# Where u times D joins the state sums of a selective scan: diagonal blocks on TensorE, or a VectorE step

## The chip, the cores and the metric

The kernel runs on one core of a Trainium2 chip. Times are device microseconds (us) of that core. The engines are TensorE (PE, with its weight loads shown as PEld), VectorE (DVE), ScalarE (ACT), GpSimd (POOL) and SyncE (SP), which issues the DMAs. SBUF is the memory on the chip, PSUM the banks into which TensorE writes its products.

## The reference

A decoder layer on x of 16 batches x 256 positions x 512 features, in three stages, each followed by a residual add and a layer norm: a selective scan, a cross-attention of 16 heads, and a gated feed-forward network (FFN) with ternary weights. What the change touches is the end of the scan stage. For each batch, with 1024 channels d, 16 states n and 256 positions l:

```
hs   = silu(conv(x W_in_states))              # (d, l), called u in the kernel
dA   = exp(A[d,n] * dt[d,l])
s    = dA * s + dt * B[n,l] * hs              # scan over l, for every d and n
y    = sum over n of s[d,n,l] * C[n,l]
y    = y + hs * D[d]
y    = y * silu(gate)
out  = y W_out
```

The line `y + hs * D` is the one whose place moves.

## The kernel before

**Tiling.** Batches go one after the other in the code (`prep`, `scan`, `attn`, `ffn` for each b), but the instructions of several batches lie beside each other: a planner orders them. The 1024 channels are eight tiles of 128 (d = 0 to 7). In the scan a tile is split into four groups g of 32 channels; a group spreads its 32 channels times 4 state rows over 128 partitions, and 4 state columns times 256 positions over the free dimension, so that one buffer h of 128x1024 holds all 16 states of 32 channels.

**One group of the scan** (the loop over g in `scan`): a DMA fetches dt and dt*u into a buffer `dtr` (L654); GpSimd multiplies B into it (`first`, through the helper `product`, L233; some of batch 0's on VectorE, L661); ScalarE makes the decays into a PSUM buffer `dA` (L668, twice two of them); VectorE runs the recurrence (L672, two scans of 128x512); GpSimd multiplies by C (`weigh`, L233 again). So a tile takes eight GpSimd products and eight VectorE scans.

**The end of a tile.** Task `sums` on TensorE takes a PSUM bank `pb` and adds up: first four blocks of 32x32, one for each group, whose diagonal holds D (`diag`, L694), times u; then 16 products with the selector `sel`, which add the state rows and columns of the four h buffers (L697). It frees the four h buffers. The first sums wait for the last `weigh`. Task `gate` on VectorE multiplies the bank by the gate z into u (L705) and frees the bank. After four tiles the output projection reads u (L736). `diag` is made once, in the setup (L326).

A float32 product appears in the trace as two records, so a tile has 8 records of L694 and 32 of L697.

**Order.** Every step is a task with an engine, a due time and an estimated duration: `task(t, engine, us, fn, after, take, free)`. The function `run` simulates the five queues (PE, DVE, ACT, POOL, SP) in these planner units and issues, for an idle engine, the ready task with the earliest due time whose buffers are free, as long as that due time is within AHEAD of the earliest task not begun. The chip then executes each engine's queue strictly in the order so written. The due times are sums of constants at the head of the file (SCAN, WEIGHP, SUMP and GATE for the scan; PREP, PSTEP, SOFT and SSTEP for the stage before; OUT0, ATT, SLAG, NORM and LNF for the attention; FFN and FDN for the FFN; WQ0 and WQ for the start and step of the 24 weight-quantising tasks, L439 and L441). Batches are due 32 units (NSL) apart. Buffers come from rings of fixed size (h has 7, dtr 4, dA 2, five general PSUM banks).

Other lines that are named later: L517 is the convolution's step on VectorE, L520 its end; L845 the row maxima of the attention; L889 its exponentials on ScalarE; L896 its weighted values; L830 its scores; L491 and L544 projections; L763 and L766 the attention's projections and their bias; L1013, L1023 and L1025 the FFN's upper half, L1086 and L1089 its lower; L458 and L459 the layer norm's statistics.

Of the kernel before, what the change touches and what calls it, by code (L numbers as in the profile page):

```python
# [10 lines left out]
F32 = mybir.dt.float32  # L11
# [4 lines left out]
ALU = mybir.AluOpType  # L16
# [4 lines left out]
P = 128  # L21
L = 256
H = 512
DI = 1024
NS = 16
NDT = DI // P
# [13 lines left out]
NB4 = 4  # L40
DB = P // NB4
# [1 line left out]

PREP = -24.16
SOFT = -7.09
SSTEP = 9.0
VUNITS = 24
GATE = -0.34
OUT0 = 25.01
OUT1 = 34.11  # L50
PSTEP = 2.02
TSP = 15.44
BCP = 9.29
KP = 34.45
QP = 37.76
VP = -3.68
SUMP = 0.16
WEIGHP = 1.88
FSTEP = 0.74
FUP = -0.18  # L60
BACK = 0.59

SHIFT = [(0, 0, 0, 0, 0, 0)] * 16
FDN = 14.54
LNF = 7.28
ATT = 39.73
SLAG = 7.79
GSTEP = 3.93
SCAN = -0.29
NORM = 81.05  # L70
FFN = 98.49
WQ = 3.57
WQ0 = 21.99
WS = 0.66
WS0 = 14.23
AHEAD = 12.29
HOP = 0.2
RINGS = {
    "xT": 2, "win": 2, "wr": 1, "wout": 1, "u": 4, "tmp": 2, "z": 2, "s": 3, "ts": 1, "bc": 1, "bcr": 3, "dtr": 4, "h": 7,
# [7 lines left out]
def decoder_kernel(ctx, tc, x, xT, ctx_in, mask, winT, wdtT, wbcT, wdpT, woutT, dvec, wqkvT, bqk, bv, wguT, wdnT, out):  # L87
    nc = tc.nc
# [16 lines left out]
    def const(shape, dt, s):  # L105
        return cp.tile(shape, dt, tag=s, name=s)
# [37 lines left out]
    def task(t, eng, us, fn, after=(), take=(), free=(), kb=0):  # L144
        if any(h.tag == "ps" for h in free) and eng in ("DVE", "ACT"):
            t -= BACK
        k = Task()
        k.t, k.i, k.eng, k.us, k.fn, k.take, k.free, k.kb = t, len(tasks), eng, us, fn, take, free, kb
        k.then, k.begun = [], False
        k.left = len(after)  # L150
        for p in after:
            p.then.append(k)
        for h in take:
            h.first = k
        for h in free:
            h.users += 1
        tasks.append(k)
        return k
# [104 lines left out]
    def cut(t, a, b):  # L263
        return t.rearrange("p (a b) -> p a b", a=a, b=b)
# [4 lines left out]
    dv = cut(free["pT"][0][:, : NDT * 23], NDT, 23)  # L269
# [14 lines left out]
    sel = const([P, DB], F32, "sel")  # L284
# [36 lines left out]

    sel4 = const([P, 2 * NS], F32, "sel4")
    nc.vector.tensor_reduce(sel4, ident.rearrange("p (g m) -> p m g", m=2 * NS), AX.X, ALU.add)
    diag = const([P, NDT, 2 * NS], F32, "diag")
    for d in range(NDT):
        nc.vector.tensor_scalar(diag[:, d, :], sel4, dv[:, d, 5:6], None, ALU.mult)  # L326
    wbc_t = const([P, NDT, 2 * NS], F32, "wbc")
    wqkv_t = const([P, 2, 768], F32, "wqkv")

# [70 lines left out]
    def setup_w():  # L400
# [33 lines left out]
        for j in range(24):  # L434
            t = WQ0 + WQ * j
            h, q = Hold("hq"), Hold("fw")
# [57 lines left out]
    def prep(b):  # L494
# [9 lines left out]
        for d0 in range(0, NDT, 2):  # L504
            t = T + PREP + PSTEP * d0
            hw, t_w = load_win(t - 5, d0 * P) if b else load_win(T + PREP - 3 + 0.1 * d0, d0 * P, "h")
# [72 lines left out]
        for hf in range(2):  # L579
            t = T + SOFT + SSTEP * hf  # L580
            ds = (4 * hf, 4 * hf + 2)
# [32 lines left out]
    def scan(b):  # L614
        st = S[b]
        T = b * NSL + SHIFT[b][1]
        st["t_y"] = []
        J = NS // NB4
        if b == 0 and VUNITS:

            hb = Hold("ps", 2)

            def spread():
                for i in range(2):
                    nc.scalar.copy(hb.t[i], st["B"].t[:, i * H : (i + 1) * H])

            t_hb = task(T - 2, "ACT", 1.1, spread, (st["t_B"],), (hb,), (st["B"],))


        hx, t_x = st["xT"]  # L630
        st["z"], st["t_z"] = [], []
        for i in range(4):
            d0, t = 2 * i, T + 8 * i + GATE
            hw, t_w = load_win(t - 5, DI + d0 * P)
            pb, z = Hold("ps"), Hold("z")

            def silu(pb=pb, z=z):
                nc.vector.scalar_tensor_tensor(z.t, z.t, 1.0, pb.t, ALU.add, ALU.mult)

            m = task(t, "PE", 3.45, lambda pb=pb, hw=hw: project(pb.t, hx, hw), (t_x, t_w), (pb, z), (hx, hw))  # L640
            m = task(t, "ACT", 0.53, lambda pb=pb, z=z: nc.scalar.activation(z.t, pb.t, AF.Tanh, scale=0.5), (m,))
            st["z"].append(z)
            st["t_z"].append(task(t, "DVE", 0.61, silu, (m,), (), (pb,)))
        for d in range(NDT):
            hs, ws = [], []
            for g in range(NB4):
                k = NB4 * d + g
                t = T + k - SCAN
                hd, hh = Hold("dtr"), Hold("h")
                hs.append(hh)  # L650

                def fetch(d=d, g=g, hd=hd):
                    src = st["dtd"][d, DB * g : DB * g + DB].rearrange("c k l -> c (k l)")
                    nc.sync.dma_start(out=hd.t, in_=src.unsqueeze(1).broadcast_to([DB, NB4, 2 * L]))  # L654

                def first(hd=hd, hh=hh):
                    product(cut(hh.t, J, L), cut(st["B"].t, J, L), hd.t[:, None, L : 2 * L].broadcast_to([P, J, L]))

                def first_v(hd=hd, hh=hh):
                    for i in range(2):  # L660
                        nc.vector.tensor_tensor(  # L661
                            cut(hh.t, J, L)[:, 2 * i : 2 * i + 2, :], cut(hb.t[i], 2, L), hd.t[:, None, L : 2 * L].broadcast_to([P, 2, L]), ALU.mult
                        )

                def decay(h2, ha, hd=hd, d=d, g=g):
                    for i in range(2):
                        j = 2 * h2 + i
                        nc.scalar.activation(ha.t[:, i, 1:], hd.t[:, 1:L], AF.Exp, scale=A[:, d, g, j : j + 1])  # L668

                def run_(h2, ha, hh=hh):  # L670
                    seg = hh.t[:, 2 * h2 * L : 2 * (h2 + 1) * L]
                    nc.vector.tensor_tensor_scan(seg, ha.t.rearrange("p n l -> p (n l)"), seg, 0.0, ALU.mult, ALU.add)  # L672

                def weigh(hh=hh):
                    st["hC"] = product(hh.t, hh.t, st["C"].t)

                f = dma(t - 4, fetch, (st["t_dt"][d // 2],), (hd,), (), 256)
                if b == 0 and k % 2 and k < VUNITS:
                    p1 = task(t - 0.75, "DVE", 1.2, first_v, (f, t_hb), (hh,), (hd, hb))
                else:  # L680
                    p1 = task(t - 0.75, "POOL", 2.34, first, (f, st["t_B"]), (hh,), (hd, st["B"]))
                rs = []
                for h2 in range(2):
                    ha = Hold("dA")
                    a = task(t - 0.6 + 0.5 * h2, "ACT", 0.92, lambda h2=h2, ha=ha, f=decay: f(h2, ha), (f,), (ha,), (hd,))
                    rs.append(task(t + 0.5 * h2, "DVE", 1.14, lambda h2=h2, ha=ha, f=run_: f(h2, ha), (a, p1), (), (ha,)))
                ws.append(task(t + WEIGHP, "POOL", 2.34, weigh, tuple(rs) + (st["t_C"],), (), (st["C"],)))
            pb = Hold("ps")

            def sums(hs=hs, pb=pb, d=d):  # L690

                for g in range(NB4):
                    r = slice(DB * g, DB * g + DB)
                    nc.tensor.matmul(pb.t[r, :L], diag[r, d, :], st["u_of"](d)[r, :], start=True, stop=False, tile_position=(DB * g, DB * g))  # L694
                for j in range(J):
                    for g in range(NB4):
                        m = nc.tensor.matmul(  # L697
                            pb.t[DB * g : DB * g + DB, :L], sel, cut(hs[g].t, J, L)[:, j, :], start=False, stop=j == J - 1, tile_position=(0, DB * g)
                        )
                        if j == 0 and g < NB4 - 1:  # L700
                            after(m, st["hC"])

            def gate(pb=pb, d=d):
                u = st["u_of"](d)
                nc.vector.tensor_tensor(u, pb.t[:, :L], st["z"][d // 2].t[:, d % 2 * L : (d % 2 + 1) * L], ALU.mult)  # L705

            m = task(T + 4 * d + 4 + SUMP, "PE", 2.45, sums, tuple(ws), (pb,), tuple(hs))
            st["t_y"].append(task(T + 4 * d + 4.25 + SUMP, "DVE", 0.42, gate, (m, st["t_z"][d // 2]), (), (pb, st["z"][d // 2])))


    def attn(b):
# [81 lines left out]
        for s in range(4):  # L793
            t = T + att + SLAG + VP + 0.7 * s
            pb = Hold("ps")
# [18 lines left out]
        def heads(g):  # L814
# [69 lines left out]
            for c in range(4):  # L884
                t = T0 + c * gstep / 4 + SLAG
                hp = Hold("pT")
# [40 lines left out]
        no = (n0, n1)  # L927
        t = T + NORM + SHIFT[b][4]
        SO = tuple(t_so)
# [29 lines left out]
    def ffn(b):  # L959
# [74 lines left out]
        for t in range(2):  # L1034
# [60 lines left out]
            t_d.append([task(Et + 1, "DVE", 0.74, add, (m,), (), (pb, ho))])  # L1095
        t_e = layernorm(E + LNF, hr, t_d)
        dma(E + LNF + 0.5, lambda: nc.sync.dma_start(out=out[b].rearrange("(k p) h -> p k h", p=P), in_=x2()), tuple(t_e), (), (hr,), 512)

# [78 lines left out]
```

## Time and profile before

| | |
|---|---|
| median of 3 runs | 3010.79 us (3008.86 to 3011.28) |
| the profiled execution | 3007.98 us, of which the span of instructions is 3005.8 us |
| granted TensorE clock, mean | 0.965 |
| VectorE scans, L672 | 1024 of 1208 ns, 1223.3 us |
| GpSimd products of the scan, L233 | 1012 of 2363 ns, 2385.6 us |
| diagonal blocks, L694 | 1024 records, 84.9 us |
| sums, L697 | 4096 records, 262.0 us |
| gate, L705 | 128 of 413 ns, 52.8 us |

How to read a profile's rows: a group is "line engine operation out<-in shapes xcount | busy us, mean ns of one | idle time of the engine before them <- who ended it". Records of an engine can overlap, so busy times of groups can add up to more than an engine's busy time. A wait is written "who <- for whom: us in total, times, longest us". A row of a timeline is "start, duration, engine, line, operation, x how many in a row"; a bracket gives the idle time before it. The chain is followed back from the last instruction: at each step to what released it, or to the instruction before it on the same engine.

### The profile page before, as it was taken

To read this page: it belongs to the slowest core of one execution; us is meant where nothing else is said; L and a number is where in the kernel's file an instruction comes from. 1 tells how busy PE (TensorE), PEld (TensorE's weight loads), DVE (VectorE), ACT (ScalarE), POOL (GpSimd) and SP (SyncE) were. 2 spreads that over 40 slices of the span, in tenths; PEclk is the share of its full clock that TensorE was granted. 3 is DMA by queue.
4 is the path that set the end of the run, shared out by engine and by line. 5 is a ranking of instruction groups with operands and counts; after the bars stand their busy time and mean duration, and the time that the engine had idled before them with its cause. 6 is when DMAs were issued, how large, how long until landed. Compare 5 with 4: busy or idle time off the path is not lost.

```text
span 3005.8 us, 51881 instructions
## 1 busy us (share of the span) xinstructions
PE 2650.5 (88%) x17514; PEld 1319.4 (44%) x17514; DVE 2674.1 (89%) x4043; ACT 2334.0 (78%) x4731; POOL 2596.5 (86%) x1435
## 2 busy tenths in 40 slices
PE   6567888999989999898999989899998999999995
PEld 4333443454545445444444544444353544434333
DVE  6969888999989999898999989899999989999873
ACT  4787978787787878778787877878788787888674
POOL 3899999999898999989899998989989899999311
PEclk9787999999999999999999999999999999999998
DMA  6695776566465665746665574656646566564432
GB/s 215 222 305 182 233 224 205 188 199 206 143 218 182 204 195 171 224 138 214 193 200 186 168 224 150 216 189 196 189 157 226 165 203 193 187 203 147 125 98 71
DMA packets 363250, 567.46 MB, mean 189 GB/s; under 512 B 47316, under 2 KB 200024, under 8 KB 358888
## 3 DMA queue, kind: packets, MB, share of 16 engines
q1 hardware_dynamic: 362984, 564.16, 58.2%
q8 instruction: 137, 2.24, 0.3%
q14 instruction: 129, 1.06, 0.1%
HBM read 449.61 MB, written 114.43 MB: 188 GB/s over the span
## 4 chain that ended last, share of the span: by engine, by line
POOL 28%; PE 27%; DVE 16%; ACT 13%; issue 10%; DMA 5%; SPq 1%; POOLq 0%; ACTq 0%; DVEq 0%
POOL h L233 23%; DVE h L672 7%; PE bank L491 6%; ACT pT L889 4%; PE bank L697 4%; DVE mx L845 4%; PE av L896 3%; PE bank L830 3%; ACT dA L668 3%; PE bank L1013 3%; PE bank L763 2%; PE bank L799 2%; DMA dtr<-dtd 2%; ACT xres L469 1%; POOL s L233 1%
## 5 line engine op out<-in xcount | busy, mean ns | idle before, releaser
L672 DVE TENSOR_TENSOR_SCAN h<-dA,h 128x512 f32<-128x512 f32 x1024 | 1223.3, 1208 | 83.0 <-POOL h L233 41.2
L233 POOL TENSOR_TENSOR h<-h,bcr 128x1024 f32<-128x1024 f32 x512 | 1207.9, 2363 | 95.7 <-DVE h L672 92.9
L233 POOL TENSOR_TENSOR h<-bcr,dtr 128x1024 f32<-128x1024 f32 x500 | 1177.7, 2363 | 69.9 <-PE bank L697 63.4
L668 ACT ACTIVATE dA<-dtr,A 128x255 f32<-128x255 f32 x2048 | 963.9, 475 | 297.1 <-DVE h L672 255.6
L830 PE MATMUL bank<-qk 108*128 108x512 bf16 x2003 | 616.3, 385 | 78.9 <-DVE mx L845 44.7
L845 DVE TENSOR_REDUCE mx<-bank 128x1 f32<-128x512 f32 x1004 | 655.1, 675 | 25.8 <-PE bank L830 25.6
L889 ACT ACTIVATE pT<-bank 128x512 f32<-128x512 f32 x999 | 566.6, 590 | 119.1 <-PE bank L830 113.9
L491 PE MATMUL bank<-xT,win 128*128 128x256 f32 x1984 | 454.5, 382 | 20.4 <-DVE u L520 7.8
L896 PE MATMUL av<-pT,vaug 128*32 128x256 f32 x4096 | 336.2, 397 | 106.6 <-ACT pT L889 104.5
L491 PEld LDWEIGHTS bank<-xT,win 128*128 128x128 f32 x1984 | 377.2, 192 | 83.8 <-DVE u L520 9.5
L830 PEld LDWEIGHTS <-qk 108*128 108x128 bf16 x2048 | 179.7, 98 | 392.2 <-issue 264.2
L697 PE MATMUL bank<-h,sel 128*32 128x256 f32 x4096 | 262.0, 399 | 49.0 <-POOL h L233 48.9
L1013 PE MATMUL bank<-fw,xqT 128*128 128x512 fp8e4 x976 | 248.5, 381 | 12.5 <-DVE hq L1023 4.0
L896 PEld LDWEIGHTS av<-pT,vaug 128*32 128x32 f32 x4096 | 88.8, 109 | 356.8 <-ACT pT L889 277.9
L736 PE MATMUL bank<-wout,u 128*128 128x512 f32 x512 | 231.0, 595 | 4.9 <-DVE u L705 4.4
L697 PEld LDWEIGHTS bank<-h,sel 128*32 128x32 f32 x4096 | 124.1, 114 | 180.9 <-POOL h L233 72.2
L517 DVE SCALAR_TENSOR_TENSOR tmp<-bank,cw,tmp 128x254 f32<-128x254 f32 (+2 forms) x384 | 165.1, 468 | 7.8 <-ACT tmp L510 7.7
L1013 PEld LDWEIGHTS <-xqT 128*128 128x128 bf16 x1024 | 96.3, 98 | 151.4 <-issue 57.6
L736 PEld LDWEIGHTS bank<-wout,u 128*128 128x128 f32 x512 | 96.0, 190 | 108.5 <-issue 94.4
L1086 PE MATMUL bank<-fw,s 128*128 128x512 fp8e4 x496 | 127.0, 380 | 1.8 <-ACT s L1077 1.1
L233 POOL TENSOR_TENSOR s<-s,u 128x512 f32<-128x512 f32 x64 | 80.7, 1272 | 39.9 <-ACT s L595 39.9
L705 DVE TENSOR_TENSOR u<-bank,z 128x256 f32<-128x256 f32 x128 | 52.8, 413 | 60.9 <-PE bank L697 60.8
(157 smaller groups left out, 2961.7 us busy)
## 6 DMA issues: line engine op xcount, KB each, us to landing
dtr<-dtd SPq DMA_DIRECT2D x512, 256.0 KB
win<-in_winT SPq DMA_DIRECT2D x124, 512.0 KB
qk<-sqk SPq DMA_DIRECT2D x128, 384.0 KB
dtd<-s SPq DMA_DIRECT2D x64, 512.0 KB
wout<-in_woutT SPq DMA_DIRECT2D x32, 1024.0 KB
fw<-gu_q SPq DMA_DIRECT2D x64, 512.0 KB
sqk<-qf SPq DMA_DIRECT2D x64, 384.0 KB
bcr<-bcd SPq DMA_DIRECT2D x32, 512.0 KB
```

What stands on the lines that cost most here:

```text
L233: return nc.gpsimd.tensor_tensor(out, a, b, ALU.mult)
L491: nc.tensor.matmul(ps_t[:, i * L : (i + 1) * L], ws[:, k, i * P : (i + 1) * P], xt[:, k, :], start=k == 0, stop=k == 3)
L517: nc.vector.scalar_tensor_tensor(zi, pb.t[:, i * L : (i + 1) * L - s], cw[:, d0 + i, j : j + 1], zi, ALU.mult, ALU.add)
L668: nc.scalar.activation(ha.t[:, i, 1:], hd.t[:, 1:L], AF.Exp, scale=A[:, d, g, j : j + 1])
L672: nc.vector.tensor_tensor_scan(seg, ha.t.rearrange("p n l -> p (n l)"), seg, 0.0, ALU.mult, ALU.add)
L697: m = nc.tensor.matmul(pb.t[DB * g : DB * g + DB, :L], sel, cut(hs[g].t, J, L)[:, j, :], start=False, stop=j == J - 1, tile_position=(0, D ...
L736: nc.tensor.matmul(pb.t, u[:, i, lt * P : (lt + 1) * P], wo()[:, i, :], start=i == 0, stop=i == 3)
L830: nc.tensor.matmul(pb.t, qk()[:, j, side, c * P : (c + 1) * P], qk()[:, j, 1 - side, :], start=True, stop=True)
L845: task(t, "DVE", 0.62, lambda pb=pb, c=c, j=j: nc.vector.tensor_reduce(mx()[:, j, c : c + 1], pb.t, AX.X, ALU.max), (m,), (), (pb,))
L889: V["x"] = nc.scalar.activation(hp.t[:, j * H : (j + 1) * H], pb.t, AF.Exp, scale=DSC)
L896: i = nc.tensor.matmul(hav.t[32 * k : 32 * k + 32, :], vaug_f[:, c, c0 : c0 + 32], hp.t[:, j * H + h * L : j * H + (h + 1) * L], start=c == 0,
L1013: nc.tensor.matmul(pb.t, xqT()[:, i, t * P : (t + 1) * P], wu()[:, k, i, :], start=i == 0, stop=i == 3)
```

## The change

The blocks `diag` and their products go. The setup keeps a copy `Dv` of D instead. `gate` has one more VectorE instruction: the bank becomes u * D + bank, in place, and then the old product with z reads it. The first sum of each group now opens the accumulation. The planner's estimates change with it (2.45 to 2.15 for `sums`, 0.42 to 0.8 for `gate`), and so do the values of 12 of its constants.

```diff
-SSTEP = 9.0
+SSTEP = 9.03
-GATE = -0.34
+GATE = -0.86
-PSTEP = 2.02
+PSTEP = 2.15
-WEIGHP = 1.88
+WEIGHP = 1.62
-LNF = 7.28
+LNF = 7.02
-SLAG = 7.79
+SLAG = 7.6
-SCAN = -0.29
-NORM = 81.05
+SCAN = -0.28
+NORM = 83.06
-WQ = 3.57
-WQ0 = 21.99
-WS = 0.66
+WQ = 1.8
+WQ0 = 27.91
+WS = 0.73
-AHEAD = 12.29
+AHEAD = 15.57
...
-    diag = const([P, NDT, 2 * NS], F32, "diag")
-    for d in range(NDT):
-        nc.vector.tensor_scalar(diag[:, d, :], sel4, dv[:, d, 5:6], None, ALU.mult)
+    Dv = const([P, NDT], F32, "Dv")
+    nc.vector.tensor_copy(Dv, dv[:, :, 5])
...
             def sums(hs=hs, pb=pb, d=d):
-
-                for g in range(NB4):
-                    r = slice(DB * g, DB * g + DB)
-                    nc.tensor.matmul(pb.t[r, :L], diag[r, d, :], st["u_of"](d)[r, :], start=True, stop=False, tile_position=(DB * g, DB * g))
                 for j in range(J):
                     for g in range(NB4):
                         m = nc.tensor.matmul(
-                            pb.t[DB * g : DB * g + DB, :L], sel, cut(hs[g].t, J, L)[:, j, :], start=False, stop=j == J - 1, tile_position=(0, DB * g)
+                            pb.t[DB * g : DB * g + DB, :L], sel, cut(hs[g].t, J, L)[:, j, :], start=j == 0, stop=j == J - 1, tile_position=(0, DB * g)
                         )
...
             def gate(pb=pb, d=d):
                 u = st["u_of"](d)
+                nc.vector.scalar_tensor_tensor(pb.t[:, :L], u, Dv[:, d : d + 1], pb.t[:, :L], ALU.mult, ALU.add)
                 nc.vector.tensor_tensor(u, pb.t[:, :L], st["z"][d // 2].t[:, d % 2 * L : (d % 2 + 1) * L], ALU.mult)
 
-            m = task(T + 4 * d + 4 + SUMP, "PE", 2.45, sums, tuple(ws), (pb,), tuple(hs))
-            st["t_y"].append(task(T + 4 * d + 4.25 + SUMP, "DVE", 0.42, gate, (m, st["t_z"][d // 2]), (), (pb, st["z"][d // 2])))
+            m = task(T + 4 * d + 4 + SUMP, "PE", 2.15, sums, tuple(ws), (pb,), tuple(hs))
+            st["t_y"].append(task(T + 4 * d + 4.25 + SUMP, "DVE", 0.8, gate, (m, st["t_z"][d // 2]), (), (pb, st["z"][d // 2])))
```

## The prediction

> **What bounds the kernel now.** I read the page first, for the loads and for the chain that ended last.
>
> ```profile
> PE 2650.5 (88%) x17514; PEld 1319.4 (44%) x17514; DVE 2674.1 (89%) x4043; ACT 2334.0 (78%) x4731; POOL 2596.5 (86%) x1435
> ...
> POOL 28%; PE 27%; DVE 16%; ACT 13%; issue 10%; DMA 5%; SPq 1%; POOLq 0%; ACTq 0%; DVEq 0%
> ```
>
> Three engines lie within three per cent of each other, and the chain passes between them. No single engine sets the time, so an average says nothing; the place decides. The first gate (L705) of each batch in the timeline lies at 74.4, 220.7, 381.2, 550.1, 724.4 us and so on to 2672.1: batches 0 to 2 take 146, 161 and 169 us, and from batch 3 on each takes 174.3 to 178.5 us, mostly 177.1. So I cut one steady batch in two and asked for the engines' busy time in each half (columns: length, PE, PEld, DVE, ACT, POOL, clock, DMA share, GB/s).
>
> ```profile
> 1610.60:1699.20 88.60, 83.95 (x552) 45.00 (x548) 86.16 (x140) 68.46 (x139) 78.47 (x40) 1.00 0.57 180
> 1699.20:1787.70 88.50, 78.64 (x554) 36.70 (x546) 78.47 (x109) 72.32 (x152) 85.40 (x52) 0.98 0.63 200
> ```
>
> In the first half VectorE is busy 97% and GpSimd loses 10.1 us; in the second GpSimd is busy 96% and VectorE is idle for 10.0 us. The waits of GpSimd in the first half say for whom:
>
> ```profile
> POOL h L233 <- DVE h L672: 6.0, 2, 4.8
> POOL h L233 <- PE bank L697: 4.4, 2, 3.5
> ```
>
> First for scans that stand in VectorE's queue (L672), then for sums on TensorE that must free the h buffers (L697). The same view of the second half has one wait of 1.2 us for a scan and one of 1.0 us for the sums. The four gates at 1610.6, 1631.2, 1655.1 and 1676.0 us lie in VectorE's half, the other four (from 1701.9 us) in GpSimd's. That division carries the forecast.
>
> **Price of the TensorE part.** 128 tasks lose eight matmul records each (four blocks, each float32 product in two records). One of them, and the sums behind it:
>
> ```profile
> 1607.91 0.63 PE L694 MATMUL bank<-u,diag 32*32 32x256 f32 x8
> 1608.48 1.93 PE L697 MATMUL bank<-h,sel 128*32 128x256 f32 x32
> ```
>
> The first sum starts 0.57 us after the first block (median of all 128: 0.56). The 32 records start over 1.93 - 0.38 = 1.55 us, that is 0.22 us for four side by side, so two such rounds would be 0.44 us; the other 0.12 is lost at the change of shape. The Trainium skill (TensorEngine Tiling (Array Packing), Key Properties) says that changing the tiling mode drains TensorE; by it one of two changes of mode remains, and 0.44 us goes rather than 0.56. I take the row's 0.56 and keep 0.44 as its lower end: 128 x 0.56 = 72 us of TensorE's queue (56 to 72), 4.5 us a batch. Where TensorE waits between blocks and sums, the blocks were free already: that is so in 19 of the 128, by over 0.1 us.
>
> **Price of the VectorE part.** One SCALAR_TENSOR_TENSOR of 128x256, PSUM and SBUF in, a pointer scalar, PSUM out, in front of each L705. No such row exists; the nearest are:
>
> ```profile
> L517 DVE SCALAR_TENSOR_TENSOR tmp<-bank,cw,tmp 128x255 f32<-128x255 f32 x128 | 56.5, 468 | 7.7 <-ACT tmp L510 7.7
> L705 DVE TENSOR_TENSOR u<-bank,z 128x256 f32<-128x256 f32 x128 | 52.8, 413 | 60.9 <-PE bank L697 60.8
> L766 DVE SCALAR_TENSOR_TENSOR bank<-bank,bqk,mb 128x512 f32<-128x512 f32 x64 | 47.8, 747 | 14.1 <-PE bank L763 14.1
> L1089 DVE SCALAR_TENSOR_TENSOR xres<-bank,fod,xres 128x512 f32<-128x512 f32 x31 | 22.9, 740 | 13.9 <-PE bank L1086 13.8
> ```
>
> L517 gives 468 ns; the output in PSUM adds 747 - 740 = 7 ns: 0.48 us. What matters is how far it pushes the queue:
>
> ```profile
> 1514.07 0.66 DVE L458 BATCH_NORM_STATS2 lst<-xres 128x6 f32<-128x512 f32 x1
> 1514.76 0.18 DVE L459 BATCH_NORM_AGGREGATE lmv<-lst 128x2 f32<-128x6 f32 x1
> ...
> 1519.04 0.86 DVE L517 SCALAR_TENSOR_TENSOR tmp<-bank,cw,tmp 128x254 f32<-128x254 f32 x2
> ```
>
> Two independent L517 take 0.86 us together, 0.39 apart, since neighbours overlap by some 0.08. A pair in which the second reads the first's result (L458, L459) doesn't overlap: it leaves 0.03 us open. The new pair is of that kind, so a gate costs 0.48 + 0.03 = 0.51 us (ends 0.39 and 0.56, as if overlapped, or with a second gap). 128 x 0.51 = 65 us, 4.1 us a batch. Setup trades eight L326 of 237 ns for one small copy (L272, 171 ns), 1.7 us less of VectorE at 4 to 8 us, under the first weights' DMA and product: nothing, and -1.7 us if that cover were gone.
>
> **What lands on the path.** Of the four gates in VectorE's half all 4 x 0.51 = 2.04 us push the scans behind them (behind a gate stand L672, L517 or L845; GpSimd's weighing waits for the scan, ScalarE's decay for its dA buffer). Against that, a gate which now waits for its sums is released earlier. VectorE's waits for L697 in this half are 2.0 us in three gates: 0.65 at 1610.6, where the blocks were in TensorE's way (gives back 0.56); 1.2 at 1631.2, where the sums themselves waited for GpSimd, so nothing; 0.16 at 1676.0. That returns 0.72. Net 2.04 - 0.72 = 1.3 us a batch. GpSimd's longest wait for sums, at 1675.9, could shrink by 0.56, but it waits for VectorE once more after that (1.16 us at 1700.5), so what it gains there it loses again. In GpSimd's half the four gates fit into 10.0 us of idle VectorE: nothing; if that idle time could not be used, 2.0 us a batch. Batches 0 to 2 and the last one are like that half throughout (171 us windows from 70 to 412 and 2635 to 2806 us: GpSimd 159.7 to 165.1 us): nothing. Behind the last gate (2804.6 us) come 200 us of attention and FFN without scans, moved by 0.51 - 0.56: nothing. So 12 batches x 1.3 = +16 us.
>
> The weighed rule: the trace's steady row has VectorE as the fullest engine, 164.6 of 177.1 us. The Trainium skill (Perfetto Trace Analysis, Identifying the Most-Contended Engine) tells to relieve the engine of highest occupancy first, and not to read TensorE by its matmul busy share. By that rule the change goes the wrong way, and all of the 65 us would count. The halves above say that only the share in VectorE's half counts.
>
> **Moved constants.** The task times, due times and AHEAD feed a list planner, so the order of all five queues is drawn anew, SP's DMA issues included. The trace can price this only by its own variation: steady batches, whose orders differ, take 174.3 to 178.5 us, about +-2 us, so +-24 us over 12. I take 0 and keep both ends. Quantising the weights (L439, L441: 24 pairs between 184 and 619 us, step 19 us) gets half the step; ScalarE is at 197 of 240 us there (187 to 427 us) and would go to some 220, still under GpSimd's 227: 0, with perhaps 15 us if decays are held up.
>
> **Sum.** The profiled execution took 3007.98 us (span 3005.8). +16 gives 3024; the median of the three runs is 2.8 higher, so 3027. About 0.2%, 6 us, is the least that a measurement of this kernel can tell from no change.
>
> **Rivals.**
> - *VectorE bounds throughout* (slower, 0.18). If the new order evens out the halves, every gate counts: 65 us less what earlier sums return. In the trace 46 gates wait though their sums ran without a wait; the smaller of 0.56 and each wait sums to 21 us. So +44, up to +65: 3055 to 3076. For it: 164.6 + 4.1 = 168.7 of 177.1 us. Against: 10 us idle in one half.
> - *TensorE's queue was the path* (faster, 0.27). In the chain followed piece by piece, L694 holds 27.7 us in 344 pieces and L705 only 7.1 us in 23. Keep that chain and take 27.7 out, put 23 x 0.51 = 12 in: -16, 2995, down to 2983 if the additions hide. It decides if TensorE frees h buffers earlier (GpSimd's 63.4 us of waits for L697, 29 times) and VectorE's delay doesn't come back to GpSimd. Against: 6.0 of the 10.4 us in VectorE's half are waits for scans.
> - *Both cancel* (same, 0.13): 16 us is also what 29 x 0.56 of shorter GpSimd waits would return; 3011.
>
> The forecast itself, +6 to +35 us, has 0.42. So faster 0.27, same 0.13, slower 0.42 + 0.18 = 0.60. The range, 2988 to 3068, leaves out about one in ten on each side: a full 27.7 us gain or a new order that helps, and VectorE's full price.
>
> **What would show it.** Right: the added row near 480 ns, gap to L705 about 0.03 us; VectorE near 168 us per steady batch, period 178 to 179; GpSimd's waits for scans (92.9 us) higher and for sums (63.4) lower; gates waiting less than 60.8 us in all. Wrong: a period below 176 us with GpSimd's waits for scans no longer than before means TensorE was the limit; above 180, that VectorE is. A time moved outside batches 3 to 14 would mean that the moved constants, not the gate, made the difference.

## The result, and the profile after

The changed kernel takes 3062.51 us (median of 4 runs, 3059.38 to 3067.52) against 3011.03 us: 1.0174 times the time before, with a 95% interval of 1.016 to 1.0189, so 51 us slower. The direction and the range held; the forecast of 16 us is a third of what was lost. The profiled execution took 3059.38 us, 3057.6 us of it the span.

The loads and the chain from the page of the changed kernel:

```profile
PE 2613.8 (85%) x16490; PEld 1311.3 (43%) x16490; DVE 2729.1 (89%) x4164; ACT 2336.8 (76%) x4733; POOL 2597.8 (85%) x1435
...
DVE 28%; PE 24%; POOL 19%; DMA 10%; ACT 9%; issue 9%; SPq 0%; POOLq 0%; ACTq 0%; DVEq 0%
```

VectorE has 55 us more, GpSimd the same work as before (2597.8 against 2596.5), and VectorE has taken GpSimd's place at the head of the chain. VectorE's added operation costs what was forecast. The row of the added step, and one gate in the timeline of VectorE:

```profile
L700 DVE SCALAR_TENSOR_TENSOR bank<-u,Dv,bank 128x256 f32<-128x256 f32 x127 | 60.7, 478 | 73.3 <-PE bank L692 73.2
```

```profile
1681.75 0.49 DVE L700 SCALAR_TENSOR_TENSOR bank<-u,Dv,bank 128x256 f32<-128x256 f32 x1 [0.97 <-PE bank L692]
1682.27 0.42 DVE L701 TENSOR_TENSOR u<-bank,z 128x256 f32<-128x256 f32 x1
1682.61 0.68 DVE L841 TENSOR_REDUCE mx<-bank 128x1 f32<-128x512 f32 x1
```

The step takes 478 ns, and the product that depends on it starts 0.03 us after the step ends, while the next, independent instruction overlaps the product by 0.08. From step to product it is 0.516 us in the median, against the 0.51 taken.

A steady batch now takes 180.9 us instead of 176.8 (mean from first gate to first gate over batches 3 to 14). Its two halves in the windows view (PE, PEld, DVE, ACT, POOL as before), and GpSimd's waits in the first half:

```profile
1635.20:1725.60 90.40, 80.88 (x509) 43.12 (x508) 85.36 (x136) 65.56 (x134) 74.01 (x35) 1.00 0.53 159
1725.60:1816.10 90.50, 79.21 (x531) 38.08 (x530) 83.96 (x123) 75.94 (x158) 89.23 (x56) 0.98 0.65 211
```

```profile
POOL h L233 <- DVE h L671: 12.0, 6, 4.1
POOL h L233 <- PE bank L692: 4.1, 2, 2.0
```

In the second half the view shows no such wait at all. In this batch the loss is in the half that was VectorE's: GpSimd's idle time grew there from 10.1 to 16.4 us, and in the other half it fell from 3.1 to 1.3. Waits for scans have doubled in the first half, from 6.0 to 12.0 us; waits for sums are about the same. Over the whole span these waits were 92.9 and 63.4 us before and are now:

```profile
POOL h L233 <- DVE h L671: 145.0, 75, 4.1
POOL h L233 <- PE bank L692: 62.8, 35, 3.8
```

Twelve steady batches of 4.1 us are 49 of the 52 us of span. The stretch behind the last gate is unchanged (199.9 us, before 201.2), and so is the start: the first gate of batch 3 lies at 549.4, before at 550.1 us.

One account serves for everything that follows. GpSimd's busy time is 163.7 to 164.2 us a steady batch in all kernels measured here, so a batch takes 164 us plus GpSimd's waits. Summed from the trace over batches 3 to 14, by the engine that ended them, in us a batch:

| kernel | order | u D by | batch | waits for VectorE | waits for TensorE |
|---|---|---|---|---|---|
| before | old | blocks | 176.8 | 6.9 | 4.3 |
| changed | new | step | 180.9 | 11.1 | 4.3 |

(What is missing to the sum are gaps below 0.1 us.)

### The profile page after: what moved, and what is told of

It reads as the page before. It is cut to its first block, busy times and chain, and to the rows that moved or that the text cites. A ratio compares the mean times of both kernels' runs of the same rounds, so it can differ in the third digit from the quotient of the medians.

```text
span 3057.6 us, 49919 instructions
## 1 busy us (share of the span) xinstructions
PE 2613.8 (85%) x16490; PEld 1311.3 (43%) x16490; DVE 2729.1 (89%) x4164; ACT 2336.8 (76%) x4733; POOL 2597.8 (85%) x1435
## 4 chain that ended last, share of the span: by engine, by line
DVE 28%; PE 24%; POOL 19%; DMA 10%; ACT 9%; issue 9%; SPq 0%; POOLq 0%; ACTq 0%; DVEq 0%
POOL h L233 15%; DVE h L671 12%; DVE mx L841 7%; PE bank L490 6%; PE bank L692 4%; DMA qk<-sqk 4%; ACT pT L885 3%; PE av L892 3%; PE bank L826 3%; PE bank L795 2%; DMA out<-xres 2%; ACT dA L667 2%; DVE hq L1021 2%; DVE tmp L516 1%; DVE hq L1019 1%
## 5 line engine op out<-in xcount | busy, mean ns | idle before, releaser
L233 POOL TENSOR_TENSOR h<-h,bcr 128x1024 f32<-128x1024 f32 x512 | 1209.8, 2366 | 147.7 <-DVE h L671 145.0
L233 POOL TENSOR_TENSOR h<-bcr,dtr 128x1024 f32<-128x1024 f32 x500 | 1177.9, 2366 | 69.6 <-PE bank L692 62.8
L826 PE MATMUL bank<-qk 108*128 108x512 bf16 x1995 | 631.3, 391 | 115.8 <-DVE mx L841 32.9
L841 DVE TENSOR_REDUCE mx<-bank 128x1 f32<-128x512 f32 x1001 | 658.5, 674 | 55.6 <-PE bank L826 54.6
L490 PE MATMUL bank<-xT,win 128*128 128x256 f32 x1984 | 462.1, 387 | 15.8 <-DVE hq L1021 5.6
L892 PE MATMUL av<-pT,vaug 128*32 128x256 f32 x4096 | 343.4, 403 | 112.1 <-ACT pT L885 111.4
L692 PE MATMUL bank<-h,sel 128*32 128x256 f32 x4064 | 280.8, 423 | 115.2 <-POOL h L233 105.0
L692 PEld LDWEIGHTS bank<-h,sel 128*32 128x32 f32 x4064 | 132.5, 120 | 259.0 <-POOL h L233 160.2
L700 DVE SCALAR_TENSOR_TENSOR bank<-u,Dv,bank 128x256 f32<-128x256 f32 x127 | 60.7, 478 | 73.3 <-PE bank L692 73.2
L233 POOL TENSOR_TENSOR s<-s,u 128x512 f32<-128x512 f32 x64 | 81.3, 1280 | 40.4 <-ACT s L594 39.6
```

The costliest lines, as they stand in the source:

```text
L233: return nc.gpsimd.tensor_tensor(out, a, b, ALU.mult)
L490: nc.tensor.matmul(ps_t[:, i * L : (i + 1) * L], ws[:, k, i * P : (i + 1) * P], xt[:, k, :], start=k == 0, stop=k == 3)
L692: m = nc.tensor.matmul(pb.t[DB * g : DB * g + DB, :L], sel, cut(hs[g].t, J, L)[:, j, :], start=j == 0, stop=j == J - 1, tile_position=(0, ...
L826: nc.tensor.matmul(pb.t, qk()[:, j, side, c * P : (c + 1) * P], qk()[:, j, 1 - side, :], start=True, stop=True)
L841: task(t, "DVE", 0.62, lambda pb=pb, c=c, j=j: nc.vector.tensor_reduce(mx()[:, j, c : c + 1], pb.t, AX.X, ALU.max), (m,), (), (pb,))
L892: i = nc.tensor.matmul(hav.t[32 * k : 32 * k + 32, :], vaug_f[:, c, c0 : c0 + 32], hp.t[:, j * H + h * L : j * H + (h + 1) * L], start=c == 0,
```

## Experiments: the operations, with the order held

Beside the runs that follow, the kernel before took 3009.9 to 3013.1 us (medians), so differences between kernels measured beside different runs are good to about 3 us.

The change does two things at once: it swaps an operation, and through estimates and constants it has the planner write another order. The first kernel keeps all constants and estimates of before. The instructions of ScalarE, GpSimd and SP then stand in exactly the old order, those of TensorE and VectorE too but for the blocks, the steps and a few rows of the setup.

```diff
-                for g in range(NB4):   # the four blocks, L694
...
+                nc.vector.scalar_tensor_tensor(pb.t[:, :L], u, Dv[:, d : d + 1], pb.t[:, :L], ALU.mult, ALU.add)
     "PE", 2.45, sums    "DVE", 0.42, gate    # and every constant: as before
```

> The code of the change alone: blocks out, the VectorE step in, with all constants and estimates of the kernel before, so that every queue keeps the order of before. Place theory (the prediction: the step costs 0.51 us only at the gates that lie in VectorE's half of a batch, and the blocks give back a little): 16 us more than before, about 3027. Throughout theory (every VectorE microsecond counts, whatever the order): 44 to 65 us more, 3055 to 3076. Order theory (the swap itself is nearly free, the new order made from the new constants is the worse one): 0 to 10 us more, 3011 to 3021.

Measured: 3020.15 us against 3011.56, 1.0026 (1.0015 to 1.0038), 9 us more. The whole swap is worth a sixth of the loss.

Its two sides alone. The step added, with zeros for D, blocks kept:

```diff
+    Dv = const([P, NDT], F32, "Dv")
+    nc.vector.memset(Dv, 0.0)
...
+                nc.vector.scalar_tensor_tensor(pb.t[:, :L], u, Dv[:, d : d + 1], pb.t[:, :L], ALU.mult, ALU.add)
```

> Order of before, the diagonal blocks stay, and the VectorE step is added with a column of zeros in place of D, so that it only costs time. Place theory: 4 gates x 0.51 us x 12 batches = 24 us more, 3035. Throughout theory: 65 us more, 3076. Theory that TensorE was the path and VectorE has room: 12 us more or less, 3023.

Measured: 3027.84 us, 1.0055 (1.004 to 1.007), 16 us more. The blocks left out, nothing in their place:

```diff
-                    nc.tensor.matmul(pb.t[r, :L], diag[r, d, :], st["u_of"](d)[r, :], start=True, stop=False, tile_position=(DB * g, DB * g))
...
```

> Order of before, the diagonal blocks are left out and nothing takes their place (the term u times D is missing). Place theory: 0 to 9 us less, since 0.72 us of gate waits per batch return in VectorE's half, 3002 to 3011. TensorE as the path: 16 to 28 us less, 2983 to 2995. Throughout theory: up to 21 us less, by what the gates waited for sums that ran without a wait, 2990.

Measured: 2996.43 us, 0.995 (0.9934 to 0.9967), 15 us less. So 65 us of VectorE cost 16, the blocks, priced at 72 us of TensorE, gave 15, and together they cost 9. (TensorE's busy time fell by less than the 72: by 45 us without the blocks, from 2650.5 to 2605.2, and by 50 with the swap.) The waits of GpSimd over the whole span, first of the kernel before, then of the swap, of the step alone, and without the blocks:

```profile
POOL h L233 <- DVE h L672: 92.9, 45, 4.8
POOL h L233 <- PE bank L697: 63.4, 29, 4.5
```

```profile
POOL h L233 <- DVE h L671: 115.4, 77, 4.8
POOL h L233 <- PE bank L692: 43.9, 28, 3.9
```

```profile
POOL h L233 <- DVE h L674: 110.1, 66, 4.8
POOL h L233 <- PE bank L699: 63.1, 31, 3.1
```

```profile
POOL h L233 <- DVE h L669: 95.0, 52, 4.9
POOL h L233 <- PE bank L690: 41.8, 23, 3.6
```

The step lengthens the waits for scans by some 20 us and leaves those for sums alone; leaving out the blocks shortens the waits for sums by as much and leaves those for scans alone. The swap has both. By steady batch:

| kernel | order | u D by | batch | waits for VectorE | waits for TensorE |
|---|---|---|---|---|---|
| swap alone | old | step | 177.3 | 8.6 | 3.0 |
| step added | old | both | 178.1 | 8.2 | 4.0 |
| blocks left out | old | nothing | 176.0 | 7.2 | 3.1 |

The place within a batch, next: the step in the tiles of one half, blocks in the other four.

```diff
-                for g in range(NB4):
+                for g in range(NB4 if not (d < 4) else 0):
...
+                if d < 4:
+                    nc.vector.scalar_tensor_tensor(pb.t[:, :L], u, Dv[:, d : d + 1], pb.t[:, :L], ALU.mult, ALU.add)
...
```

> Order of before; the VectorE step takes the place of the blocks in tiles 0 to 3 of each batch alone, whose gates lie in VectorE's half of a steady batch. The full swap in this order measured 9 us more than before, adding the step alone 16 more, leaving the blocks out alone 15 less. Place theory: all of the swap's loss comes from these tiles, 9 to 16 us more, 3020 to 3027. Even theory (every gate counts alike): half of 9, about 4 more, 3015. Theory that the gain from the blocks lies here: no change or less, 3005 to 3011.

> Order of before; the VectorE step in tiles 4 to 7 alone, whose gates lie in GpSimd's half. Place theory: no loss there, and what the blocks give back, 0 to 7 us less, 3004 to 3011. Even theory: about 4 us more, 3015.

Measured: tiles 0 to 3 alone 3020.02 us against 3009.9, 1.0037 (1.0024 to 1.005); tiles 4 to 7 alone (`d >= 4`) 3008.87 us, 1.0 (0.9988 to 1.0013). The same swap costs 10 us in VectorE's half and nothing in GpSimd's. Nor is the nothing two effects that cancel: by steady batch GpSimd's waits for VectorE and TensorE are 6.9 and 4.2 us with the swap in tiles 4 to 7, against 6.9 and 4.3 before, and 8.7 and 3.3 with it in tiles 0 to 3. The division on which the forecast rested holds in the old order.

## Experiments: the order

Now the other factor: all new constants and estimates, so the changed kernel's order, but with the blocks; and that order with neither blocks nor step.

```diff
+SSTEP = 9.03 ... AHEAD = 15.57           # all twelve, and 2.15 and 0.8
     diag, and its four products: kept
```

> All new constants and estimates of the changed kernel, so its order in every queue, but the diagonal blocks in place of the VectorE step. Throughout theory: the step's 46 us go, about 3011 to 3020. Order theory: the time stays within 15 us of the changed kernel's 3062, so 3047 to 3062. Place theory: 25 us or so less than the changed kernel, 3035.

> The changed kernel in its own order with the VectorE step left out (the term u times D is missing, no blocks either). Leaving out the blocks from the order of before gave 15 us, adding the step there cost 16. If the step's price depends on the place in a batch alone: 16 to 25 us less than the changed kernel, 3037 to 3046. If the new order has enough idle VectorE time to hide it: 3055 to 3062. If the step is what makes the new order slow: about 3011.

Measured: 3071.26 us with the blocks, 1.0202 (1.0187 to 1.0218); 3059.61 us with neither, 1.0158 (1.0135 to 1.0181). In the new order the step costs 3 us, hardly to be told from nothing, and the swap even gains some 9. The order costs, with operations equal: 60 us with blocks, 42 with the step (3062.51 less 3020.15), 63 with neither. GpSimd's waits of the kernel with neither:

```profile
POOL h L233 <- DVE h L669: 137.8, 72, 4.5
...
POOL h L233 <- PE bank L690: 64.2, 35, 3.4
```

Against the same operations in the old order (95.0 and 41.8, shown above without the blocks) these are 43 us more of waiting for scans and 22 more for sums, with no added work on VectorE. A steady batch of this kernel takes 181.6 us, with 11.4 of waits for VectorE and 4.3 for TensorE; with blocks 181.4, 11.0 and 5.0: the changed kernel's figures, whatever adds u times D.

Which input spoils the order? Five kernels change parts of them. The changed kernel with the two old estimates:

```diff
-"PE", 2.15, sums    "DVE", 0.8, gate
+"PE", 2.45, sums    "DVE", 0.42, gate
```

> The changed kernel with the planner's estimates of before for the two tasks (2.45 and 0.42 in place of 2.15 and 0.8), all twelve new constants kept. If the two estimates spoil the order: about 3020. If the constants do: it stays within 10 us of 3062.

The changed kernel with the nine constants of the steady order at their old values:

```diff
-SSTEP = 9.03 ... AHEAD = 15.57
+SSTEP = 9.0 ... AHEAD = 12.29            # WQ, WQ0, WS, 2.15 and 0.8 stay new
```

> The changed kernel with the nine constants of the steady order (SSTEP, GATE, PSTEP, WEIGHP, LNF, SLAG, SCAN, NORM, AHEAD) at their values of before; the new estimates and the new start of the weight quantising (WQ, WQ0, WS) stay, without which these estimates leave the planner stuck. If the nine constants spoil the order: about 3020. If the two estimates do: about 3062. If any redrawn order is worse than the one that the constants of before were found with: somewhere between 3030 and 3070.

The kernel before with the gate's estimate nudged, with NORM nudged, and with WQ, WQ0 and WS new:

```diff
-"DVE", 0.42, gate        # c1        -NORM = 81.05     # n3        -WQ = 3.57, WQ0 = 21.99, WS = 0.66    # h
+"DVE", 0.46, gate                    +NORM = 81.3                  +WQ = 1.8, WQ0 = 27.91, WS = 0.73
```

> The kernel before, with no operation changed: only the planner's estimate of the gate goes from 0.42 to 0.46, which redraws the order (some 1500 of 4037 VectorE instructions move). Redraw theory (the constants of before were found together with its order, and another order made from nearly the same inputs loses what the changed kernel lost): 20 to 60 us more, 3030 to 3070. Theory that the particular new constants are bad, and any nearby order is as good: within 8 us of 3011.

> The kernel before with NORM 81.3 in place of 81.05 alone, no operation changed (some 360 VectorE instructions move). Redraw theory: 5 to 40 us more, since fewer move. Theory that nearby orders are as good: within 8 us of 3011.

> The kernel before with the new start and step of the weight quantising alone (WQ, WQ0, WS), no operation changed. The prediction took 0, with 15 us if ScalarE's decays are held up: 3011 to 3026. Redraw theory: 5 to 40 us more, by the later batches too and not only by the first three.

| kernel | us | ratio, 95% interval |
|---|---|---|
| new constants, old estimates | 3059.05 | 1.016 (1.0141 to 1.0178) |
| new estimates, old steady constants | 3080.56 | 1.0238 (1.0223 to 1.0254) |
| before, gate's estimate 0.46 | 3040.51 | 1.0088 (1.0065 to 1.011) |
| before, NORM 81.3 | 3020.11 | 1.0022 (1.0011 to 1.0032) |
| before, WQ, WQ0, WS new | 3012.67 | 1.0001 (0.9991 to 1.0011) |

No single input is the culprit. New constants spoil the order without the estimates, the estimates spoil it without the constants, and 0.04 on one estimate, with not one operation changed, costs 28 us. Only the new times of the weight quantising (WQ, WQ0, WS) cost nothing, as forecast. Nor do the worse orders lose in one place: a steady batch of the kernel with 0.46 takes 179.1 us, with 6.8 of waits for VectorE and 6.5 for TensorE, so its loss lies with the sums, that of the changed kernel's order mostly with the scans. The order of before is a good one among neighbours that are worse. The runs don't say how rare it is.

## Experiments: what in the new order costs

First theory: long stretches of other work on VectorE, runs for short. In the written order of a steady batch VectorE has four stretches of over 5 us of attention, FFN and convolution work between two scans, before there were two; GpSimd can run ahead only as far as the h buffers go. A rule in the planner breaks them:

```diff
+                todo = wait[e]
+                if e == "DVE" and since[0] > 2.5:      # other work since the last scan
+                    todo = sorted(todo, key=lambda w: (w[2].us != 1.14, w[0], w[1]))
...
```

> The changed kernel, same operations, constants and estimates, with one rule more in the planner: when VectorE has done over 2.5 units of other work since the last scan, a ready scan goes first. In the order so written no run of other work between scans is over 4.5 us in a steady batch (6.8 in the changed kernel). Clump theory: GpSimd's waits for scans fall below 7 us a batch, and the time to 2995 to 3030. Theory that TensorE's or the DMAs' order is the cause: within 15 us of 3062.

> The same rule, constants and estimates with the diagonal blocks in place of the VectorE step (without the rule this order measured 3071). Clump theory: 2990 to 3030. If breaking the runs helps and the step costs 9 to 16 us as in the order of before, it is that much faster than its sister with the step. Other theory: 3055 to 3075.

Measured: 3081.6 us with the step, 1.0231 (1.0212 to 1.0249), and 3072.64 with the blocks, 1.0196 (1.0171 to 1.022). The runs were gone (none over 4.8 us from the second steady batch on with the step, 5.0 with the blocks), the lost time was not: runs alone don't explain it. What they cost with every other queue in place isn't shown, since the rule redraws those too. The waits with the rule and the step:

```profile
POOL h L238 <- DVE h L676: 131.9, 92, 4.1
...
POOL h L238 <- PE bank L697: 88.9, 45, 4.1
```

Waits for scans are a little shorter than the changed kernel's 145.0 but more numerous (92 against 75), and those for sums are 26 us longer (before the rule 62.8). The loss had moved.

Then load. If an engine's queue were too full in the new order, taking work from it with every queue in place would close the gap. VectorE: the row maxima over half their columns.

```diff
-nc.vector.tensor_reduce(mx()[:, j, c : c + 1], pb.t, AX.X, ALU.max)
+nc.vector.tensor_reduce(mx()[:, j, c : c + 1], pb.t[:, :L], AX.X, ALU.max)
```

> The kernel before, order kept in every queue, but each of the 64 row maxima of a batch (L845, 0.675 us) reads 256 columns of 512, some 0.27 us less each, 17 us of VectorE a batch. If VectorE's runs cost the old order only its 6 to 7 us of GpSimd waits a batch: 50 to 90 us less than before, 2920 to 2960. GpSimd's own 164 us a batch bounds it.

> The changed kernel, its order kept, with the same half maxima. Clump theory: the gap to the old order (52 us) shrinks, since VectorE's runs get shorter: within 25 us of the sister run with the old order. Theory that TensorE's or the DMAs' order is the cause: the gap stays at 40 to 55 us.

Measured: 2987.49 us in the old order, 0.9921 (0.99 to 0.9942), and 3027.42 in the new, 1.0049 (1.003 to 1.0068). Over 200 us of VectorE's work (its busy time falls from 2674.1 to 2449.1 us) buy 26 us in the old order and 35 in the new; the expectation of 50 to 90 missed. The gap between the orders, 51 us without this, stays at 40. GpSimd's waits, old order, then new:

```profile
POOL h L233 <- PE bank L697: 69.2, 41, 3.5
POOL h L233 <- DVE h L672: 66.5, 42, 4.2
```

```profile
POOL h L233 <- DVE h L671: 115.1, 60, 4.3
...
POOL h L233 <- PE bank L692: 61.3, 37, 2.7
```

In the new order GpSimd still waits 115 us for scans although VectorE has much less to do. VectorE's own two longest waits in that kernel are for TensorE, for the attention's scores and for the sums:

```profile
DVE mx L841 <- PE bank L826: 105.5, 130, 3.8
DVE bank L700 <- PE bank L692: 85.9, 67, 5.5
```

In the old order the same two are 54.6 and 79.8 us. A scan that stands in the queue behind such an instruction is held up with it; that this is what makes the scans late is an inference, no run shows it by itself.

TensorE: the FFN's upper products over a quarter of the features. Its busy time falls by 94 us in the old order (2650.5 to 2556.4).

```diff
-                    for i in range(4):
+                    for i in range(1):
-... start=i == 0, stop=i == 3)
+... start=i == 0, stop=i == 0)
```

> The kernel before, order kept, with the FFN's upper products (L1013) summed over a quarter of the features: 3 of 4 records of 0.215 us pace left out in 16 tasks, 10.4 us of TensorE a batch less, 166 us in all. Leaving out the blocks (72 us of TensorE) gave 15, so at that rate 35 us less: 2978. If TensorE is not what this stretch waits for: 0 to 10 less.

> The changed kernel, order kept, with the same products left out. If TensorE's queue carries what the new order loses: 55 to 85 us less, within 20 us of the sister run with the old order. If the loss is in the order of the work itself, whatever engine is relieved: the gap to the sister stays at 40 to 55 us.

Measured: 3008.2 us in the old order, 0.9988 (0.9976 to 1.0), and 3056.43 in the new, 1.0163 (1.0124 to 1.0202). Next to nothing in either; the gap is 48 us. So the new order isn't slow because VectorE or TensorE is overfull; ScalarE's queue and the DMAs' were not lightened. With the operations equal, what differs is which task stands behind which, and GpSimd, at whose pace a batch runs, gets its scans later. Which of the moved tasks do it stays open; neither breaking the runs nor lightening a queue found them.

One mark of the new order is followed up by no run. TensorE's scores wait for the DMA that brings their operands, in the kernel before and in the changed one:

```profile
PE bank L830 <- DMA qk<-sqk: 3.0, 3, 2.5
```

```profile
PE bank L826 <- DMA qk<-sqk: 18.5, 13, 2.0
```

With neither blocks nor step the new order has 31.8 us of it, the old one 6.7. SyncE's queue, which issues the DMAs, was redrawn with the others. It can't be the whole cause: the kernel with new estimates and old steady constants, the slowest but one, has 7.1.

## Why the prediction was right or wrong

**The prices.** VectorE's were right: 478 ns against 0.48 us, a gap of 34 ns against 0.03, VectorE 168.3 us a batch (1346.68 us in the eight batches from 1273.9 us) against "near 168". TensorE's 72 us were not measured as queue time; its busy time fell by 45 to 50 us in the old order.

**The place.** Right in kind: tiles 0 to 3 cost 10 us, tiles 4 to 7 nothing. The size was 16 us against 9 for the whole swap. Two terms were off. Waits of GpSimd for scans rose by 1.7 us a batch (6.9 to 8.6) where 1.3 was taken, but its waits for sums fell by 1.3 (4.3 to 3.0), and the sentence "what it gains there it loses again" had set that to nothing. Per batch the swap cost 0.5 instead of 1.3. In the two profiled executions, whose spans are 11.4 us apart, 6.0 lie in the twelve steady batches, 3.4 ahead of them and 1.9 behind, and those ends were held for covered.

**"Moved constants ... I take 0 and keep both ends".** This is the step that failed. The order measures +42 us with the step and +60 with the blocks, outside the +-24 of the text. The direction was right mostly by luck: 9 of the 51 us are the swap's, the rest is this term's. The bound came from the spread of steady batches, 174.3 to 178.5 us. The prediction takes the orders of these batches to differ. In the trace of before that holds for the first two alone, which are the two ends of the spread: from batch 5 on VectorE runs the same 247 instructions in every batch, in an order that changes by the place of one. So these batches are one plan settling into a period; they say nothing of other plans. A nudge of 0.04 to one estimate moved the mean batch to 179.1, outside that spread. Nothing in the trace of before shows another order, so no row could have priced this; the sum should have shown it as an unknown with a wide upper end. Its sign came out of the runs alone: the neighbouring orders with 0.46 and with NORM 81.3 are slower, and none tried is faster.

**The rivals.** "VectorE bounds throughout" had 3055 to 3076, and the measured time lies in it, for another reason: the step costs 16 us in the old order and 3 in the new, and the changed order without any step still takes 3060. That the time fell into this range is luck. The text's own sign, a period above 180 us meaning that VectorE is the limit, would have misled: 180.9 us came about in an order in which 229 us less of VectorE's work (2729.1 to 2500.3) bought 35. "TensorE's queue was the path" has its mechanism shown at fixed order (15 us for the blocks alone, just under the 16 to 28), but it is undone by the step. The weighed rule of the Trainium skill (Perfetto Trace Analysis, Identifying the Most-Contended Engine) names VectorE, the fullest engine before and after (164.6 of 177.1, 169.3 of 180.9 us), with GpSimd close behind at 163.9 before; relieving VectorE with the order kept paid about a ninth (26 of 225 us), so place outweighed occupancy here.

**The signs.** With the old order two of them came true: GpSimd's waits for sums fell to 43.9 us, and the gates waited 30.1 us in all instead of 60.8. In the changed kernel GpSimd's waits for sums hardly moved (62.8), and the gates waited longer, 73.2 us (the row of L700). The last sentence of the signs pointed the right way: a time that the gate doesn't explain tells of the constants. Only, it was looked for outside batches 3 to 14, and it lay inside them.

## What to carry to other kernels

A change that feeds a planner is two changes: swap the operation with the old order written down first, measure that, and only then let the order move; here that separates 9 us from 42. Where one engine has the same work in every version, write the time as its work plus its waits: the waits, by releaser and by place, say what an edit did, while occupancies of 90% on three engines don't. A price that the trace can't hold, such as that of an order not yet drawn, belongs into the range with its full width, not into the sum as zero.

## What the runs showed of the hardware

With a quarter of the FFN's upper products TensorE's clock was lower: the mean granted clock fell from 0.965 to 0.945 in the old order and from 0.956 to 0.939 in the new; in the old order's steady batches it read 0.97 against 0.99. The score products (L830) that stayed took 393 ns in the mean instead of 385, so a part of the work taken away came back as slower work. The Trainium skill (TensorE: Matmul & The Clock Gate, Part 1) says that the gate follows recent activity of the array, which agrees; what part came back in this way was not measured.

The 2.36 us products of GpSimd were the same with 225 us less or 55 us more on VectorE: GpSimd's busy time stayed at 2596 to 2599 us in the kernels shown here.
